# Two non-local attention layers in float32: who reads the products of a small matrix inverse out of PSUM

## The chip, the cores and the metric

The kernel runs on one core of one Trainium2 chip. The metric is the time of one execution on the device, in microseconds. All data are float32.

## The reference

Two layers of the same form follow each other on an image batch x of 4 x 128 x 96 x 96. Cut to what matters, one layer is:

```python
g_x = maxpool2(conv1x1(x, g_w, g_b))        # 64 channels, 2304 keys
theta_x = conv1x1(x, theta_w, theta_b)      # 64 channels, 9216 queries
phi_x = maxpool2(conv1x1(x, phi_w, phi_b))  # 64 channels, 2304 keys
attn = softmax(theta_x^T phi_x, over keys)
y = attn g_x
W_y = conv1x1(y, W_w, W_b)                  # back to 128 channels
inv = bn_gamma * rsqrt(bn_var + 1e-5)
return W_y * inv + (bn_beta - bn_mean * inv) + x
```

## The kernel before

**The work.** There are eight blocks (4 images, 2 layers), and each goes through its 9216 queries in nine pairs of 512 + 512. For a pair the kernel walks over 18 tiles of 128 keys: TensorE makes scores (`scores`, line L927, PSUM tile `sc`), ScalarE takes their exponential into SBUF (L932, `exp`), VectorE adds the exponentials up for the denominators (L939 and L941, `sum`), and TensorE multiplies them by the values (`values`, L949, PSUM tile `av`). One main loop runs over 648 *slots* `t`; a slot handles two key tiles, so nine slots make a pair, and 18 slots (`CYCLE`) are a cycle of two pairs. Each slot writes out, in this order: scores of tile 0, a piece of side work called `first`, scores of tile 1, a piece called `second`, the two additions to the sum, the values of the slot before, and then `closes`. Every engine runs its own instructions in the order written (no scheduler moves them).

**Side work.** Keys, values and queries of the next block are made beside the attention of the present one, by a `Unit` of eight steps `split`, `second` ... `eighth` at slots 8, 9, 11, 12, 14, 17, 20, 23 of a cycle (matmuls L685 and L694, PSUM tile `unit_ps`). Of interest below is `sixth_sum` (L764 to L771): three VectorE instructions, L766, L767, L770, read the two PSUM tiles of `sixth`. At slot 10 of a cycle a `theta_alone` also needs two PSUM tiles.

**The two banks.** All side work shares one PSUM pool, `ps_misc`, of two banks. `two_banks` hands out both at once, and whoever comes next on TensorE has to wait until the engine that reads the earlier products is done with them.

**The inverse.** The 128 x 64 projection W of each layer, scaled by the batch norm, has an upper 64 x 64 half A. `Fold` computes B = A^-1 times the other half by Newton's iteration, for both layers at once, 14 rounds, in slots 16 to 90, so that from the second block on the projection needs half the matmuls. One round is a `half` (V = I - A X / 2, one product per layer) and a `whole` (X = 2 c X V, four small products). Then come `first` (B = X times the right half), `residual`, `mended` (a correction of B), and `residual` again. `NEWTONS` lists the slots; at a listed slot, `whole` stands in the place of `first`, and the next `half` in `closes`, behind the values. In the profile the tiles of `Fold` carry the name `x`, since they are slices of the buffer of a later image.

Before, each `half` and each `whole` takes two new banks; ScalarE reads the products of `whole` (L379), and VectorE those of `half`, with the -0.5 and the identity in one instruction for each layer (L358). VectorE also reads the products of `residual` (L410) and `mended` (L416).

**W's loads.** `load_W` (L191 to L195) issues two DMAs on SyncE's queue for each layer, both layers ahead of the loop. VectorE scales W in `make_scale` (L210) at slot 9.

Of the kernel before, what the change touches and what calls it, by code (L numbers as in the profile page):

```python
# [11 lines left out]
AF = mybir.ActivationFunctionType  # L12
ALU = mybir.AluOpType
# [4 lines left out]
B, C, CI, H, W = 4, 128, 64, 96, 96  # L18
# [51 lines left out]
def shifted_blocks(ctx: ExitStack, tc: tile.TileContext, x: bass.AP, layers, out: bass.AP, flag):  # L70
# [24 lines left out]
    nc = tc.nc  # L95
# [17 lines left out]
    ident = const.tile([P, P], F32, name="ident")  # L113
# [5 lines left out]
    ones = const.tile([P, CI], F32, name="ones")  # L119
# [21 lines left out]
    def slice_of(n):  # L141
        used[0] += n
        return third[:, used[0] - n : used[0]]
# [154 lines left out]
    class Fold:  # L298


        def __init__(self):
            self.X = [slice_of(CI) for _ in range(2)]
            self.V, self.rest, self.square = (slice_of(CI) for _ in range(3))
            self.B = [slice_of(CI) for _ in range(2)]
# [13 lines left out]
        def squares(self, l):  # L318
            A = ws[l].W_bn[:CI, :]
            nc.vector.tensor_tensor(self.square[:CI, :], A, A, op=ALU.mult)  # L320
            nc.vector.tensor_reduce(self.total[:CI, l : l + 1], self.square[:CI, :], AX.X, ALU.add)
            nc.scalar.copy(self.X[l][ts(1 - l, CI), :], A)

        def begin(self, name):
            self.pss = two_banks(f"fold_ps_{name}")

        def scale(self):
            self.begin("scale")
            ps = self.pss[0][:, :2]
            for h in range(2):  # L330
                nc.tensor.matmul(
                    ps[ts(h, CI), :], lhsT=ones[:CI, :], rhs=self.total[:CI, :],
                    start=True, stop=True,
                )
            nc.vector.reciprocal(self.alpha, ps)

        def init(self):
            for l in range(2):
                own, other = self.own(l)
                for rows, src in ((own, self.left(l)), (other, self.X[l][other, :])):  # L340
                    nc.scalar.activation(
                        self.X[l][rows, :], src, AF.Identity, scale=self.alpha[rows, l : l + 1]
                    )
                nc.scalar.copy(self.own_alpha[own, :], self.alpha[own, l : l + 1])

        def half(self, k):

            def step():
                self.begin(f"half_{k}")
                for l in range(2):  # L350
                    own, other = self.own(l)
                    nc.tensor.matmul(
                        self.pss[l][other, :CI], lhsT=self.left(l), rhs=self.X[l][own, :],
                        start=True, stop=True,
                    )
                for l in range(2):
                    own, other = self.own(l)
                    nc.vector.scalar_tensor_tensor(  # L358
                        self.V[other, :], self.pss[l][other, :CI], -0.5, ident[other, other],
                        op0=ALU.mult, op1=ALU.add,  # L360
                    )

            return step

        def whole(self, k, c):

            def step():
                self.begin(f"whole_{k}")
                cols = ts(1, CI)
                for first in range(2):  # L370
                    for l in range(2):
                        own, other = self.own(l)
                        Xt, V = self.X[l][other, :], self.V[other, :]
                        rows, lhsT, rhs = ((own, Xt, V), (other, V, Xt))[first]
                        nc.tensor.matmul(
                            self.pss[1 - l][rows, cols], lhsT=lhsT, rhs=rhs, start=True, stop=True
                        )
                for l in range(2):
                    nc.scalar.activation(  # L379
                        self.X[l], self.pss[1 - l][:, cols], AF.Identity, scale=2.0 * c  # L380
                    )

            return step

        def product(self, name, rhs, take):

            def step():
                self.begin(name)
                for l in range(2):
                    own = ts(l, CI)  # L390
                    nc.tensor.matmul(
                        self.pss[l][:CI, :CI], lhsT=self.X[l][own, :], rhs=rhs(l),
                        start=True, stop=True,
                    )
                for l in range(2):
                    take(l, self.pss[l][:CI, :CI])

            return step

        def residual(self):  # L400
            self.begin("residual")
            cols = ts(1, CI)
            for l, w in enumerate(ws):
                nc.tensor.matmul(
                    self.pss[l][ts(l, CI), cols], lhsT=w.W_bn[:CI, :], rhs=self.B[l][:CI, :],
                    start=True, stop=True,
                )
# [4 lines left out]
        def first(self, l, ps):  # L412
            nc.scalar.copy(self.B[l][:CI, :], ps)

        def mended(self, l, ps):
            nc.vector.tensor_add(self.B[l][:CI, :], self.B[l][:CI, :], ps)  # L416
            for h in range(2):
                nc.scalar.copy(ws[l].B[ts(h, CI), :], self.B[l][:CI, :])

        def note(self):  # L420
            rest, big = self.rest, 2.0**40
# [16 lines left out]

        def steps(self):

            low, todo = NEWTON_LOW, []
            for k in range(NEWTON):
                c = 2.0 / (1.0 + low * (2.0 - low))
                low *= c * (2.0 - low)
                todo += [self.half(k), self.whole(k, c)]
            rest = lambda l: self.rest[ts(l, CI), :]
            todo += [self.product("first", self.right, self.first), self.residual]
            todo += [self.product("mended", rest, self.mended), self.residual]
            return todo

        def together(self):
            self.begin("together")
            nc.tensor.matmul(
                self.pss[0][:1, :1], lhsT=ones[:, :1], rhs=ones[:, :1], start=True, stop=True
            )

    def columns(wanted, name, engine, rows=None):
# [756 lines left out]
    ws = [Layer(l, p) for l, p in enumerate(layers)]  # L1214
# [76 lines left out]
    def then(t, step):  # L1291
        after[t] = after.get(t, []) + [step]

    fold = Fold()
# [32 lines left out]
    for n in range(1, len(blocks)):  # L1327
        first = (n - 1) * NP * NB // CYCLE * CYCLE
# [32 lines left out]
    todo = [None] + fold.steps()  # L1361
    for t in NEWTONS:
        assert is_free(t) and t not in firsts
        firsts[t], closes[t] = todo.pop(0), todo.pop(0) if todo else None
    assert not todo and t < (NP + 2) * NB + 3
    while not is_free(t + 1):
        t += 1
    firsts[t + 1] = fold.together
    then(t + 2, fold.note)
    then(t + 3, fold.note_growth)  # L1370

# [420 lines left out]
```

## Time and profile before

| | |
|---|---|
| median of three runs | 2483.23 us (lowest 2482.7) |
| the profiled execution's own time | 2483.54 us |
| its span | 2481.6 us |
| TensorE (PE) busy | 2450.8 us, 99% of the span |
| VectorE (DVE) busy | 2069.2 us, 83% |
| ScalarE (ACT) busy | 1675.5 us, 68% |
| GpSimd (POOL) busy | 900.0 us, 36% |
| granted TensorE clock, mean | 0.997 |

The span is the time from the first to the last instruction of the program; 1.94 us of the execution's own time lie around it. A busy share is an average over the whole kernel: where an engine with a share of 99% stood idle has to be found by stretches. In the lines of the profile PE is TensorE's matmul, PEld its weight load, and "L358" is line 358 of the kernel. A line of the timeline has the start in us, the duration in us, the engine, the source line, the operation, output and inputs, and the count; where an engine stood idle before it, the idle time and who ended it follow in brackets.

### The profile page before, as it was taken

The page shows a single profiled execution, that of the slowest core. Times are in us where ns is not written, and L with a number is a line of the kernel's source. Part 1 is how long each engine was busy: PE and PEld are TensorE (multiplying, and loading weights), DVE is VectorE, ACT ScalarE, POOL GpSimd, SP SyncE. Part 2 cuts the span into 40 slices and gives each one's busy share as a digit, 9 for nine tenths or more (in the row PEclk, how much of TensorE's full clock was granted, in tenths as well). Part 3 has the DMA queues.
Part 4 walks back from the last instruction along what each step waited for, and adds up shares of the span by engine and source line. Part 5 has one row for each costly group of instructions (what it writes and reads, how often), then busy time and mean ns, then how long its engine had stood idle before and what let it go on. Part 6 is the DMA issues. An engine that isn't in the chain of part 4 may idle for free.

```text
span 2481.6 us, 59305 instructions
## 1 busy us (share of the span) xinstructions
PE 2450.8 (99%) x23629; PEld 1035.0 (42%) x23629; DVE 2069.2 (83%) x2644; ACT 1675.5 (68%) x1929; POOL 900.0 (36%) x1033
## 2 busy tenths in 40 slices
PE   9999989999999999999999999999999999999999
PEld 3544544333333333333566664333333333333333
DVE  8887878898888888888878888888887888887777
ACT  6665656766666766666666666767666676766665
POOL 0222323433334433434434344443433444422331
PEclk9999999999999999999999999999999999999999
DMA  5555655766467776767756767776755677644443
GB/s 190 88 88 111 122 115 106 123 110 112 80 103 123 137 132 127 138 123 141 133 99 100 130 127 129 130 133 115 117 86 96 117 128 129 127 93 84 84 86 64
DMA packets 199629, 283.95 MB, mean 114 GB/s; under 512 B 36262, under 2 KB 131888, under 8 KB 199344
## 3 DMA queue, kind: packets, MB, share of 16 engines
q0 software_dynamic: 101872, 137.69, 42.5%
q1 hardware_dynamic: 97304, 142.31, 19.9%
q8 instruction: 188, 3.08, 0.5%
q14 instruction: 97, 0.79, 0.1%
q10 hardware_dynamic: 168, 0.07, 0.0%
HBM read 54.07 MB, written 35.68 MB: 36 GB/s over the span
## 4 chain that ended last, share of the span: by engine, by line
PE 91%; DVE 5%; issue 1%; DMA 1%; ACT 1%; POOL 0%; DVEq 0%; ACTq 0%; POOLq 0%
PE av L949 42%; PE sc L927 42%; PE unit_ps L685 5%; DVE sum L941 3%; PE W_ps L1096 1%; ACT exp L932 1%; DMA sums<-x 1%; PE unit_ps L694 0%; PE gphi_ps L542 0%; PE W_ps L1103 0%; PE mix_ps L844 0%; DVE gT L860 0%; DMA x<-in_x_dram 0%; PE theta_ps L904 0%; DMA sum<-turned 0%
## 5 line engine op out<-in xcount | busy, mean ns | idle before, releaser
L932 ACT ACTIVATE exp<-sc,nshift 128x1024 f32<-128x1024 f32 x1296 | 1402.5, 1115 | 746.4 <-PE sc L927 719.4
L941 DVE TENSOR_TENSOR sum<-sum,exp 128x1024 f32<-128x1024 f32 x1151 | 1407.8, 1223 | 300.3 <-ACT exp L932 247.0
L927 PE MATMUL sc<-theta,phi 64*64 64x512 f32 x10224 | 1291.1, 590 | 0.0
L949 PE MATMUL av<-exp,gT 64*64 64x512 f32 x10368 | 1257.2, 591 | 0.0
L949 PEld LDWEIGHTS av<-exp,gT 64*64 64x64 f32 x10368 | 458.5, 133 | 617.6 <-issue 572.4
L927 PEld LDWEIGHTS sc<-theta,phi 64*64 64x64 f32 x10224 | 450.7, 133 | 603.6 <-issue 536.6
L654 POOL DMA_DIRECT2D sums<-x x252 | 307.1, 1652 | 415.0 <-PE unit_ps L685 258.5
L1001 POOL DMA_DIRECT2D turned<-sum x140 | 115.2, 942 | 667.0 <-DMA turned<-sum 512.8
L1014 POOL DMA_DIRECT2D sum<-turned x280 | 263.7, 1492 | 42.0 <-DMA sum<-turned 35.8
L1113 POOL DMA_DIRECT2D x<-halves x122 | 101.1, 973 | 255.8 <-ACT halves L1111 246.7
L1127 POOL DMA_DIRECT2D x<-halves x122 | 149.2, 1651 | 39.8 <-ACT halves L1123 38.8
L685 PE MATMUL unit_ps<-sums,mixed 64*64 64x384 f32 x896 | 144.6, 484 | 10.1 <-DVE x L358 7.2
L939 DVE TENSOR_TENSOR sum<-exp,exp 128x1024 f32<-128x1024 f32 x72 | 88.2, 1224 | 46.1 <-ACT exp L932 46.0
L1083 POOL DMA_DIRECT2D halves<-halves x70 | 97.7, 1395 | 4.7 <-ACT halves L956 4.5
L956 ACT COPY halves<-av 128x1024 f32<-128x1024 f32 x71 | 72.0, 1013 | 32.1 <-PE av L949 31.7
L685 PEld LDWEIGHTS unit_ps<-sums,mixed 64*64 64x64 f32 x896 | 55.5, 133 | 73.6 <-issue 37.1
L685 PE MATMUL unit_ps<-x,mixed 64*64 64x384 f32 x448 | 71.0, 484 | 0.4 <-DVE stage L730 0.4
L654 POOL DMA_DIRECT2D sums<-sums x28 | 23.2, 830 | 81.4 <-PE unit_ps L694 29.4
L1123 ACT ACTIVATE halves<-W_ps,shift 128x256 f32<-128x256 f32 x122 | 51.3, 480 | 0.0
L1088 DVE TENSOR_TENSOR halves<-halves 128x512 f32<-128x512 f32 x71 | 48.6, 685 | 0.0
L685 PE MATMUL unit_ps<-sums,gphiT 64*64 64x384 f32 x224 | 46.3, 483 | 0.0
L805 DVE TENSOR_REDUCE pooled_g<-stage 128x96 f32<-128x384 f32 x84 | 45.9, 546 | 0.0
(196 smaller groups left out, 1069.1 us busy)
## 6 DMA issues: line engine op xcount, KB each, us to landing
sums<-x POOLq DMA_DIRECT2D x252, 192.0 KB, 5.4
x<-halves POOLq DMA_DIRECT2D x244, 128.0 KB, 4.4
sums<-x SPq DMA_DIRECT2D x112, 192.0 KB
turned<-sum SPq DMA_DIRECT2D x140, 128.0 KB
turned<-sum POOLq DMA_DIRECT2D x140, 128.0 KB, 3.7
halves<-halves POOLq DMA_DIRECT2D x70, 256.0 KB, 5.5
halves<-row SPq DMA_DIRECT2D x140, 128.0 KB
out_dram<-x SPq DMA_DIRECT2D x35, 512.0 KB
```

The source lines that it names most:

```text
L654: return lambda: nc.gpsimd.dma_start(out=dst(), in_=src(), accum_op=ALU.add)
L685: nc.tensor.matmul(bank[ts(c, CI), :UN], lhsT=lhsT, rhs=rhs[:, c, :], start=True, stop=True)
L927: nc.tensor.matmul(ps[ts(c, CI), ts(h, QT)], lhsT=self.blk.keys_of(k, c, h), rhs=self.th[ts(h, CI), :], start=True, stop=True,)
L932: nc.scalar.activation(e, ps, AF.Exp, bias=nshift)
L939: nc.vector.tensor_add(self.sum, self.es[0], e)
L941: nc.vector.tensor_add(self.sum, self.sum, e)
L949: nc.tensor.matmul(self.av[ts(h, CI), ts(r, QT)], lhsT=self.blk.gT[ts(r, CI), k, :], rhs=e[ts(r, CI), ts(h, QT)], start=(k == 0), stop=(k ...
L1001: nc.gpsimd.dma_start(out=self.turned[ts(h, CI)], in_=self.sum[ts(h, CI), ts(h, QT)], accum_op=ALU.add,)
L1014: nc.gpsimd.dma_start(out=folded()[ts(i, SQ)], in_=self.turned[ts(i, SQ), ts(k, n)], accum_op=ALU.add,)
L1083: nc.gpsimd.dma_start(out=self.y, in_=self.halves[:, QT:], accum_op=ALU.add)
L1113: nc.gpsimd.dma_start(out=here[:CI, h, :], in_=top[ts(h, CI), :], accum_op=ALU.add)
L1127: nc.gpsimd.dma_start(out=here[CI:, :, ts(c, n)], in_=self.y[ts(c, CI), :].rearrange("p (h n) -> p h n", h=2), accum_op=ALU.add,)
```

## The change

- `half` has one bank's part for both layers. ScalarE takes the two products out of PSUM in one instruction, times -0.5, into V, and VectorE adds the identity to V later, from SBUF (`eye`, a copy of the identity made once).
- `whole` and the `half` behind it in the same slot share one pair of banks (`whole` the first 64 columns, `half` the second 64 of one of them); `begin` is called once a slot.
- `residual` and `mended` are read by ScalarE too, and VectorE does its addition from SBUF.
- The last steps are spread over one more slot, 94: residual at 88, correction and copies (`keep`) at 90, last residual at 94.
- Layer 1's `load_W` is issued in slot 4 of the loop.

```diff
-NEWTONS = (16, 18, 22, 25, 34, 36, 43, 52, 54, 58, 61, 70, 72, 79, 82, 88, 90)
+NEWTONS = (16, 18, 22, 25, 34, 36, 43, 52, 54, 58, 61, 70, 72, 79, 82, 88, 90, 94)
...
-        def half(self, k):
...
-                for l in range(2):
-                    own, other = self.own(l)
-                    nc.vector.scalar_tensor_tensor(
-                        self.V[other, :], self.pss[l][other, :CI], -0.5, ident[other, other],
-                        op0=ALU.mult, op1=ALU.add,
-                    )
...
+        def half(self):
+
+            ps = self.pss[1][:, ts(1, CI)]
+            for l in range(2):
+                own, other = self.own(l)
+                nc.tensor.matmul(
+                    ps[other, :], lhsT=self.left(l), rhs=self.X[own, l, :], start=True, stop=True
+                )
+            nc.scalar.activation(self.V, ps, AF.Identity, scale=-0.5)
+            nc.vector.tensor_add(self.V, self.V, self.eye)
...
         def residual(self):
...
+            nc.scalar.activation(self.rest, ps, AF.Identity, scale=-1.0)
             for l in range(2):
                 own = ts(l, CI)
-                nc.vector.tensor_sub(self.rest[own, :], self.right(l), self.pss[l][own, cols])
...
+                nc.vector.tensor_add(self.rest[own, :], self.rest[own, :], self.right(l))
+
+        def mended(self):
+            more = self.X[:CI]
+            self.product(lambda l: self.rest[ts(l, CI), :], more)
+            nc.vector.tensor_add(self.B[:CI], self.B[:CI], more)
+
+        def keep(self):
+            for l, w in enumerate(ws):
+                for h in range(2):
+                    nc.scalar.copy(w.B[ts(h, CI), :], self.B[:CI, l, :])
...
-    for w in ws:
-        w.load_W(nc.sync)
+    ws[0].load_W(nc.sync)
...
+    then(4, lambda: ws[1].load_W(nc.sync))
...
         if t in firsts:
             assert first is None and second is None
+            fold.begin(t)
             first = firsts[t]
```

TensorE, from the `half` at the end of slot 34 to the `sixth` of slot 35, with what each row waits for. Before:

```order
L352 MATMUL fold_ps_half_0_1616<-x_111,WT_620 64x64 [waits Activation_49]
L352 MATMUL fold_ps_half_1_1617<-x_111,WT_629 64x64 [waits Activation_49]
L927 MATMUL sc_0_3_16_1624<-theta_0_3_1019,phi_0_151 64x512 x4
L685 MATMUL unit_ps_0_1_0_1631<-sums_104,mixed_277 64x384 [waits DMASW6_49,DVE_49]
L685 MATMUL unit_ps_0_1_1_1632<-x_268,mixed_277 64x384 [waits DVE_49]
```

The same place after the change:

```order
L353 MATMUL fold_ps_1_1581<-x_111,WT_622 64x64 [waits Activation_49]
L353 MATMUL fold_ps_1_1581<-x_111,WT_631 64x64 [waits Activation_49]
L915 MATMUL sc_0_3_16_1618<-theta_0_3_1019,phi_0_149 64x512 [waits PE_49]
L915 MATMUL sc_0_3_16_1618<-theta_0_3_1019,phi_0_149 64x512 x3
L673 MATMUL unit_ps_0_1_0_1625<-sums_104,mixed_277 64x384 [waits DMASW6_49,PE_49]
L673 MATMUL unit_ps_0_1_1_1626<-x_266,mixed_277 64x384 [waits Activation_49]
```

The order of the matmuls is the same; the first matmuls of `sixth` waited for VectorE, which had `half`'s banks, and now wait for ScalarE.

ScalarE in slots 34 to 36, before:

```order
L932 ACTIVATE exp_0_3_14_1589<-sc_0_3_14_1584,nshift 128x1024
L379 ACTIVATE x_111<-fold_ps_whole_1_1592 128x64
L379 ACTIVATE x_111<-fold_ps_whole_0_1591 128x64
L932 ACTIVATE exp_0_3_15_1604<-sc_0_3_15_1599,nshift 128x1024
L932 ACTIVATE exp_0_3_16_1629<-sc_0_3_16_1624,nshift 128x1024
```

and after:

```order
L920 ACTIVATE exp_0_3_14_1587<-sc_0_3_14_1582,nshift 128x1024
L371 ACTIVATE x_111<-fold_ps_1_1581 128x64
L371 ACTIVATE x_111<-fold_ps_0_1580 128x64
L920 ACTIVATE exp_0_3_15_1600<-sc_0_3_15_1595,nshift 128x1024
L356 ACTIVATE x_111<-fold_ps_1_1581 128x64
L920 ACTIVATE exp_0_3_16_1623<-sc_0_3_16_1618,nshift 128x1024
```

One short instruction, L356, stands now between the second exponential of slot 34 and the first of slot 35.

VectorE in slots 34 and 35, before:

```order
L941 TENSOR_TENSOR sum_0_3_1337<-sum_0_3_1337,exp_0_3_15_1604 128x1024
L358 SCALAR_TENSOR_TENSOR x_111<-fold_ps_half_0_1616,ident 64x64
L358 SCALAR_TENSOR_TENSOR x_111<-fold_ps_half_1_1617,ident 64x64
L805 TENSOR_REDUCE pooled<-stage 128x96
L941 TENSOR_TENSOR sum_0_3_1337<-sum_0_3_1337,exp_0_3_16_1629 128x1024
L766 TENSOR_TENSOR stage<-stage,unit_ps_0_1_1_1632 128x384
L767 SCALAR_TENSOR_TENSOR stage<-unit_ps_0_1_0_1631,cols_first,stage 128x384
L770 TENSOR_TENSOR stage<-stage,unit_ps_0_1_0_1631 128x384
```

and after:

```order
L929 TENSOR_TENSOR sum_0_3_1333<-sum_0_3_1333,exp_0_3_15_1600 128x1024
L357 TENSOR_TENSOR x_111<-x_111 128x64
L793 TENSOR_REDUCE pooled<-stage 128x96
L929 TENSOR_TENSOR sum_0_3_1333<-sum_0_3_1333,exp_0_3_16_1623 128x1024
L754 TENSOR_TENSOR stage<-stage,unit_ps_0_1_1_1626 128x384
L755 SCALAR_TENSOR_TENSOR stage<-unit_ps_0_1_0_1625,cols_first,stage 128x384
L758 TENSOR_TENSOR stage<-stage,unit_ps_0_1_0_1625 128x384
```

One instruction stands in the place of two, and no longer reads PSUM. The `sixth_sum` (L766 to L770, now L754 to L758) still reads both banks of `sixth` behind it, and the `whole` of slot 36 needs those banks.

More of the change, by code (lines that the diff above doesn't have):

```diff
@@ L301, in __init__ @@
         def __init__(self):
-            self.X = [slice_of(CI) for _ in range(2)]
-            self.V, self.rest, self.square = (slice_of(CI) for _ in range(3))
-            self.B = [slice_of(CI) for _ in range(2)]
+            self.X, self.B = (
+                slice_of(2 * CI).rearrange("p (l c) -> p l c", l=2) for _ in range(2)
+            )
+            self.V, self.rest, self.square, self.eye = (slice_of(CI) for _ in range(4))
+            for h in range(2):
+                nc.scalar.copy(self.eye[ts(h, CI), :], ident[ts(h, CI), ts(h, CI)])
             self.alpha, self.own_alpha, self.total = slice_of(2), slice_of(1), slice_of(2)
@@ L321, in squares @@
             nc.vector.tensor_reduce(self.total[:CI, l : l + 1], self.square[:CI, :], AX.X, ALU.add)
-            nc.scalar.copy(self.X[l][ts(1 - l, CI), :], A)
+            nc.scalar.copy(self.X[ts(1 - l, CI), l, :], A)
         def begin(self, name):
@@ L372, in step @@
                         own, other = self.own(l)
-                        Xt, V = self.X[l][other, :], self.V[other, :]
+                        Xt, V = self.X[other, l, :], self.V[other, :]
                         rows, lhsT, rhs = ((own, Xt, V), (other, V, Xt))[first]
                         nc.tensor.matmul(
-                            self.pss[1 - l][rows, cols], lhsT=lhsT, rhs=rhs, start=True, stop=True
+                            self.pss[1 - l][rows, :CI], lhsT=lhsT, rhs=rhs, start=True, stop=True
                         )
@@ L379, in step, with product @@
                     nc.scalar.activation(
-                        self.X[l], self.pss[1 - l][:, cols], AF.Identity, scale=2.0 * c
+                        self.X[:, l, :], self.pss[1 - l][:, :CI], AF.Identity, scale=2.0 * c
                     )
             return step
[L385 to L403, printed above, removed]
+        def product(self, rhs, to):
+            pss = [self.pss[1 - l][:CI, ts(1, CI)] for l in range(2)]
+            for l in range(2):
                 nc.tensor.matmul(
-                    self.pss[l][ts(l, CI), cols], lhsT=w.W_bn[:CI, :], rhs=self.B[l][:CI, :],
+                    pss[l], lhsT=self.X[ts(l, CI), l, :], rhs=rhs(l),
                     start=True, stop=True,
@@ L408, in residual, with first @@
             for l in range(2):
-                own = ts(l, CI)
-                nc.vector.tensor_sub(self.rest[own, :], self.right(l), self.pss[l][own, cols])
[L412 to L418, printed above, removed]
+                nc.scalar.copy(to[:, l, :], pss[l])
+        def first(self):
+            self.product(self.right, self.B[:CI])
+        def residual(self):
+            ps = self.pss[0][:, :CI]
+            for l, w in enumerate(ws):
+                nc.tensor.matmul(
+                    ps[ts(l, CI), :], lhsT=w.W_bn[:CI, :], rhs=self.B[:CI, l, :],
+                    start=True, stop=True,
+                )
+            nc.scalar.activation(self.rest, ps, AF.Identity, scale=-1.0)
+            for l in range(2):
+                own = ts(l, CI)
+                nc.vector.tensor_add(self.rest[own, :], self.rest[own, :], self.right(l))
[4 more added lines that the diff above has]
+        def keep(self):
+            for l, w in enumerate(ws):
+                for h in range(2):
+                    nc.scalar.copy(w.B[ts(h, CI), :], self.B[:CI, l, :])
         def note(self):
@@ L439, in steps @@
         def steps(self):
-            low, todo = NEWTON_LOW, []
+            low, todo = NEWTON_LOW, [self.half]
             for k in range(NEWTON):
@@ L444, in steps @@
                 low *= c * (2.0 - low)
[L445 to L449, printed above, removed]
+                todo += [self.whole(c), self.half if k + 1 < NEWTON else self.first]
+            return todo + [self.residual, None, self.mended, self.keep, self.residual]
         def together(self):
-            self.begin("together")
             nc.tensor.matmul(
-                self.pss[0][:1, :1], lhsT=ones[:, :1], rhs=ones[:, :1], start=True, stop=True
+                self.pss[1][:1, :1], lhsT=ones[:, :1], rhs=ones[:, :1], start=True, stop=True
             )
@@ L1360, in shifted_blocks @@
     firsts, closes = {15: fold.scale}, {15: fold.init}
-    todo = [None] + fold.steps()
+    todo = [None] + fold.steps() + [fold.together]
     for t in NEWTONS:
         assert is_free(t) and t not in firsts
-        firsts[t], closes[t] = todo.pop(0), todo.pop(0) if todo else None
+        firsts[t], closes[t] = todo.pop(0), todo.pop(0)
     assert not todo and t < (NP + 2) * NB + 3
-    while not is_free(t + 1):
-        t += 1
-    firsts[t + 1] = fold.together
     then(t + 2, fold.note)
```

19 lines of the change are left out of this document (4 added, 15 removed).

## The prediction

> **What bounds the kernel now.** I read the busy shares first, then the same shares by stretch, and then TensorE's own timeline for the places where it stood idle.
>
> ```profile
> PE 2450.8 (99%) x23629; PEld 1035.0 (42%) x23629; DVE 2069.2 (83%) x2644; ACT 1675.5 (68%) x1929; POOL 900.0 (36%) x1033
> ...
> 60.00:440.00 380.00, 357.73 (x3474) 177.59 (x3470) 313.76 (x480) 238.71 (x311) 111.48 (x127) 0.98 0.57 105
> 440.00:2420.00 1980.00, 1979.23 (x19156) 814.11 (x19152) 1657.92 (x1999) 1362.75 (x1522) 772.95 (x881) 1.00 0.65 116
> ```
>
> The columns of the stretches are length, then busy time of PE, PEld, DVE, ACT and POOL, and the granted clock. From 440 us on TensorE is busy 1979.23 of 1980 us at clock 1.00: nothing that takes work from another engine can help there. From 60 to 440 us, which holds the inverse, it is idle for 380.00 - 357.73 = 22.27 us, and the clock is 0.98. So whatever this change is worth must come out of that stretch. These are TensorE's idle times in it (one more, 0.44 us at 67 us, lies before the inverse):
>
> ```profile
> 88.73 0.53 PE L685 MATMUL unit_ps<-sums,mixed 64*64 64x384 f32 x1 [2.29 <-DVE x L358]
> 115.44 1.12 PE L685 MATMUL unit_ps<-sums,mixed 64*64 64x384 f32 x8 [0.47 <-DVE x L358]
> 128.56 0.38 PE L694 MATMUL unit_ps<-x,mixed 64*64 64x192 f32 x2 [1.47 <-DVE x L358]
> 166.54 0.53 PE L685 MATMUL unit_ps<-sums,mixed 64*64 64x384 f32 x1 [1.45 <-DVE x L358]
> 207.17 0.58 PE L694 MATMUL unit_ps<-x,mixed 64*64 64x192 f32 x2 [4.66 <-DVE x L358]
> 247.55 0.53 PE L685 MATMUL unit_ps<-sums,mixed 64*64 64x384 f32 x1 [1.47 <-DVE x L358]
> 272.57 1.12 PE L685 MATMUL unit_ps<-sums,mixed 64*64 64x384 f32 x8 [0.48 <-DMA sum<-turned]
> 285.35 0.38 PE L694 MATMUL unit_ps<-x,mixed 64*64 64x192 f32 x2 [1.14 <-DVE x L358]
> 322.81 0.53 PE L685 MATMUL unit_ps<-sums,mixed 64*64 64x384 f32 x1 [1.47 <-DVE x L358]
> 362.72 0.38 PE L694 MATMUL unit_ps<-x,mixed 64*64 64x192 f32 x2 [4.81 <-DVE x L358]
> 401.73 0.53 PE L685 MATMUL unit_ps<-sums,mixed 64*64 64x384 f32 x1 [1.65 <-DVE x L416]
> 406.64 0.27 PE L404 MATMUL fold_ps_residual<-x 64*64 64x64 f32 x1 [0.47 <-DVE stage L770]
> ```
>
> In slot order these are slots 17, 23, 26, 35, 44, 53, 59, 62, 71, 80, 89 and 90: each the slot right behind a `half` (or behind `mended`). TensorE wants the two banks, and VectorE, which works its additions off in order, has not yet read `half`'s products. The one named a DMA (slot 59) has the size of its twin in slot 23 (0.48 and 0.47), also behind a `half`; I count it with them. The twelve sum to 21.83 us.
>
> Idle time has a second price. Behind the three longest the granted clock falls:
>
> ```profile
> 90.00:94.00 4.00, 4.00 (x28) 2.25 (x23) 3.97 (x9) 1.11 (x1) 0.94 (x1) 0.57 0.49 106
> 206.00:214.00 8.00, 6.83 (x44) 2.89 (x48) 3.66 (x5) 1.55 (x3) 0.00 (x0) 0.57 0.45 147
> 363.00:367.00 4.00, 4.00 (x32) 1.67 (x28) 2.05 (x2) 1.54 (x3) 0.00 (x0) 0.57 0.73 246
> 126.00:131.00 5.00, 3.53 (x43) 1.55 (x40) 3.71 (x5) 2.11 (x2) 0.56 (x1) 1.00 0.40 90
> ```
>
> A clock of 0.57 over 4 us is a loss of 4 x 0.43 = 1.7 us of work. The three cost 1.7, 8 x 0.43 - 1.17 / 2 = 2.9 (the 1.17 idle us inside did no work anyway), and 1.7: together 6.3 us. Behind the 1.47 us at 128.56 (last row) the clock stayed at 1.00.
>
> The Trainium skill ("TensorE: Matmul & The Clock Gate", section "HAM oscillation — how this bites in real kernels") puts the limit at idle gaps of more than about 3.4 us. By it the 2.29 us of slot 17 would have kept the full clock and the second price would be 1.7 us smaller; the row at 90 us says 0.57, so here the trace decides.
>
> **The change, term by term.** I take one place, slots 34 to 36, on VectorE and then on TensorE.
>
> ```profile
> 163.68 2.54 DVE L941 TENSOR_TENSOR sum<-sum,exp 128x1024 f32<-128x1024 f32 x2
> 166.26 0.48 DVE L358 SCALAR_TENSOR_TENSOR x<-fold_ps_half,ident 64x64 f32<-64x64 f32 x2
> 166.66 0.54 DVE L805 TENSOR_REDUCE pooled<-stage 128x96 f32<-128x384 f32 x1
> ...
> 168.25 0.54 DVE L766 TENSOR_TENSOR stage<-stage,unit_ps 128x384 f32<-128x384 f32 x1
> ...
> 169.24 0.54 DVE L770 TENSOR_TENSOR stage<-stage,unit_ps 128x384 f32<-128x384 f32 x1
> ...
> 164.06 1.03 PE L927 MATMUL sc<-theta,phi 64*64 64x512 f32 x5
> ...
> 167.24 1.28 PE L927 MATMUL sc<-theta,phi 64*64 64x512 f32 x8
> ...
> 169.81 1.28 PE L927 MATMUL sc<-theta,phi 64*64 64x512 f32 x8
> 170.67 0.27 PE L375 MATMUL fold_ps_whole<-x 64*64 64x64 f32 x2
> ```
>
> *Removed: the wait for L358.* TensorE runs out of scores at 164.06 + 1.03 = 165.09, and VectorE frees the bank at 166.54, behind two sums. ScalarE will free it instead. Its instruction is like the L379 that reads `whole` today (below, 226 ns), and in its queue stands only the exponential of the slot's second score tile, whose scores end 1.7 us of values earlier; the exponential behind it needs scores that TensorE makes after `half`. So the bank should be free about 0.3 us after `half` ends, inside the 0.86 us of scores that TensorE has left (169.81 to 170.67). I cost the 14 new ScalarE instructions at nothing; uncovered they would be 14 x 0.226 = 3.2 us, which I keep for the upper end.
>
> Each wait also costs a restart. Eight scores normally follow on each other in 0.86 us, two fours of 0.43, while the last four is listed with 0.59, so idle time is counted 0.16 us late; and the first four after the wait come in two steps, 0.25 apart. I take 0.2 us a wait. Twelve waits: 21.83 + 2.4 + 6.3 (clock) = **30.5 us** lie on the path now.
>
> *Given back: the next bank.* In slots 17, 35, 53, 71 and 89 the matmuls are those of `sixth`, and in the next slot `whole` (or `mended`) needs the banks that VectorE's L766 to L770 read. TensorE now comes earlier, but VectorE hardly does: it works without a pause from 163.68 to 169.78 and saves only its two L358, 0.40 us to the start of L805, against one addition from SBUF. The nearest row to that addition has the same shape:
>
> ```profile
> L379 ACT ACTIVATE x<-fold_ps_whole x28: 210/226/237, 96.0 to 373.7; 128x64 f32<-128x64 f32 x28
> ...
> L433 DVE TENSOR_TENSOR x<-BT x2: 216/218/221, 421.9 to 422.5; 128x64 f32<-128x64 f32 x2
> ```
>
> 218 ns as listed, somewhat less from start to start; I take 0.26 us saved (between 0.18 and 0.40). Today `whole` comes 170.67 - 166.54 = 4.13 us behind `sixth`. Without the wait `sixth` starts at 166.54 - 1.45 - 0.2 = 164.89 and `whole` is wanted at 169.02. L770 ends at 169.24 + 0.54 - 0.26 = 169.52, and 0.05 later (the distance from L358's end to the matmul) TensorE can go: 0.55 us of waiting, where 1.65 were. The other four places go by the same sum:
>
> ```profile
> 91.43 0.54 DVE L770 TENSOR_TENSOR stage<-stage,unit_ps 128x384 f32<-128x384 f32 x1
> ...
> 250.25 0.54 DVE L770 TENSOR_TENSOR stage<-stage,unit_ps 128x384 f32<-128x384 f32 x1
> ...
> 325.51 0.54 DVE L770 TENSOR_TENSOR stage<-stage,unit_ps 128x384 f32<-128x384 f32 x1
> ...
> 403.90 1.23 DVE L941 TENSOR_TENSOR sum<-sum,exp 128x1024 f32<-128x1024 f32 x1 [1.63 <-ACT exp L932]
> ...
> 406.04 0.55 DVE L770 TENSOR_TENSOR stage<-stage,unit_ps 128x384 f32<-128x384 f32 x1
> ```
>
> Slot 18: `whole` wanted at 88.73 - 2.49 + 4.13 = 90.37, free at 91.76: 1.4 us. Slots 54 and 72: wanted at 250.01 and 325.27, free at 250.58 and 325.84: 0.6 each. Slot 90: wanted at 401.73 - 1.85 + 4.13 = 404.01; L770 comes earlier by the 1.63 us in which VectorE waits for an exponential (ScalarE's copies of B no longer stand ahead of it) and by about 0.4 for L416 and L410, so free at about 404.6: 0.6 us. Together **3.7 us** come back, none long enough for the clock by the rows above.
>
> At `split` (slots 26, 44, 62, 80) and `eighth` (23, 59) nothing comes back: the bank behind them is read by ScalarE, or wanted two or more slots later. VectorE is late there, as the two waits near 4.7 us tell, but from 440 us on the same steps run with VectorE 84% busy and TensorE without a pause. With TensorE 4.9 us earlier in slot 44 I find `second_sum` of slot 45 done about 1.6 us before `theta_alone` wants its bank in slot 46, and in slot 81 about 1.1 us before `whole` of slot 82. That is the cover; each us beyond it would come back.
>
> *Moved and added elsewhere.* Fifteen score tiles now wait for a TensorE event, that of the matmul two key tiles back in the same buffer, long past: nothing. The two copies of `eye`, two ScalarE reads in `residual` and two in `mended` lie in ScalarE's 32% of idle time; `keep` puts four copies (about 1 us) between exponentials in slot 90, as `mended` did in 88. W of layer 1 moves on SyncE's queue behind loads that wait for the next image:
>
> ```profile
> 33.13 3.06 SPq L651 DMA_DIRECT2D sums<-x  x4
> ...
> 60.76 0.26 DVE L210 TENSOR_SCALAR x<-x,inv 128x64 f32<-128x64 f32 x1
> ```
>
> It will be issued near 35 us, and is first read at 60.76: some 25 us for 64 KB, nothing lost. The next image's load is issued a little under 1 us earlier, which no wait of TensorE shows a use for.
>
> **Sum.** 30.5 - 3.7 = 26.8 us off the profiled 2483.54 us: 2456.7, so **2457 us**. The median (2483.23) is 0.3 us from the profiled run, and I make no correction. That is 1.1% less, inside the 2% which I take as what a measurement of this kernel can tell from no change.
>
> **Rivals.**
> 1. *The wait moves in full.* If VectorE is no earlier at L770, or the restart costs more, the five places behind `sixth` give all their time back: 2.29 + 1.45 + 1.47 + 1.47 + 1.65 + 5 x 0.2 + 1.7 (clock at slot 17) = 11.0, while the others still gain 30.5 - 11.0 = 19.5: 2464 us. For it: VectorE is without a pause there. Against it: it would have to lose the 1.1 us that TensorE does not wait in slot 35.
> 2. *Nothing comes back,* if VectorE gets ahead by more than I count: 2483.5 - 30.5 = 2453 us. Against it: five rows of L770.
> 3. *Half clock behind what is left.* The 1.4 us in slot 18 lie between gaps that kept the clock (1.47) and one that lost it (2.29). A fall there costs 1.7 us more: 2458 us. The Trainium skill (the same page, section "Part 1: The HAM clock gate (the "warmup" mystery)") has a free-running window of about 3.4 us, by which the same gap may or may not lose the clock; the rows here cannot tell.
> 4. *W comes late, and it is slower.* SyncE works in order, and W stands behind the `sums` loads. If it landed after 60.8 us, VectorE would stop in `make_scale` with the exponentials' sums queued behind, TensorE would follow once the five exponential buffers are full, and each further us would cost one. To eat the gain of 26.8 it would have to land near 60.8 + 27 = 88 us; at 95 the time would be 2490. From 35 us on that is 60 us for 64 KB. Against it: SyncE is idle from 36 us on.
>
> **Chances.** Forecast with its give-back 0.68, rival 1 0.14, rival 2 0.08, rival 3 0.05, rival 4 0.02, something unseen 0.03. The range takes in rivals 1 to 3 with the unknown ends: low 2453 less 1 for the spread between runs, 2452; high 2464 + 3.2 (ScalarE's instructions uncovered), 2467. None of the cases reaches 2433.6, the mark of 2% faster: 0.01; slower by over 2% needs W 50 us later still: 0.01; within 2% 0.98.
>
> **What will show it.** After the change the stretch 60 to 440 us (now ending near 413) should have about 3 to 4 us of idle time on TensorE in five places, all at a `whole` or `mended` behind `sixth`, released by VectorE's L758, and none released by the new L357. The clock should stay at 1.00 through it. ScalarE's L356 should start within 0.2 us of the end of `half`. I am wrong if waits for ScalarE's L356 appear (an exponential held it up), if waits behind `split` move to slot 46 or 82, or if VectorE stops near 60 us.

## The result, and the profile after

The changed kernel takes **2455.85 us** (median of four runs), the kernel before 2484.38 us in the same comparison: a ratio of **0.9888**, with a 95% interval of 0.9869 to 0.9908. It is 1.1% faster, and 2457 was forecast. Each of the two medians counts one execution that took far longer than the rest (6744.94 and 3711.95 us); without them they are 2454.84 and 2483.23 us. The profiled execution took 2454.51 us, with a span of 2452.6.

The busy shares, and below them the two stretches that the forecast began with:

```profile
PE 2442.0 (100%) x23629; PEld 989.9 (40%) x23629; DVE 2064.4 (84%) x2629; ACT 1677.3 (68%) x1949; POOL 899.8 (37%) x1033
```

```profile
60.00:440.00 380.00, 377.47 (x3758) 219.71 (x3754) 332.93 (x493) 262.57 (x354) 125.55 (x143) 1.00 0.64 115
440.00:2420.00 1980.00, 1979.18 (x19140) 737.05 (x19136) 1657.90 (x2001) 1358.80 (x1516) 763.73 (x871) 1.00 0.64 114
206.00:214.00 8.00, 8.00 (x84) 6.23 (x80) 7.86 (x14) 5.13 (x6) 4.53 (x5) 1.00 0.62 84
```

In the stretch of the inverse TensorE is now idle for 380.00 - 377.47 = 2.53 us, where it was 22.27, and its clock is 1.00 instead of 0.98 (the third row is a stretch of time in which 0.57 stood before; the changed kernel is further on in its work there). From 440 us on TensorE is busy without a pause in both, 1979.18 and 1979.23 us of 1980. That alone does not say that the work there takes equally long; the starts of the exponentials below do.

The view of waits sums up who released TensorE there. First the kernel before, then the changed one; the columns are the total in us, the number of waits, and the longest:

```profile
PE unit_ps L694 <- DVE x L358: 12.1, 4, 4.8
PE unit_ps L685 <- DVE x L358: 7.2, 5, 2.3
PE unit_ps L685 <- DVE x L416: 1.6, 1, 1.6
PE unit_ps L685 <- DMA sum<-turned: 0.5, 1, 0.5
PE fold_ps_residual L404 <- DVE stage L770: 0.5, 1, 0.5
PE unit_ps L685 <- DVE stage L730: 0.4, 1, 0.4
```

```profile
PE fold_ps L367 <- DVE stage L758: 1.3, 4, 0.7
PE fold_ps L380 <- DVE stage L758: 0.7, 1, 0.7
PE unit_ps L673 <- DVE stage L718: 0.4, 1, 0.4
```

The 0.4 us at L673 (once L685) lie at 67 us, before the inverse. All waits for `half`'s reader are gone, and the five that were forecast have come, at a `whole` (L367) or `mended` (L380) behind the last read of `sixth_sum` (L758, once L770). The two new instructions are in the groups by line:

```profile
L356 ACT ACTIVATE x<-fold_ps 128x64 f32<-128x64 f32 x14 | 3.2, 225 | 4.1 <-PE fold_ps L353 4.1
L357 DVE TENSOR_TENSOR x<-x 128x64 f32<-128x64 f32 x14 | 3.1, 221 | 2.1 <-ACT x L356 2.1
```

Both last what the forecast took from their neighbours (226 and 218 ns), and no wait of TensorE's matmuls names either.

Where the time went can be followed slot by slot, by the start of a slot's first exponential in the two traces. These rows are slot 16, slot 100 and the last slot, 647, before and after:

```profile
83.64 1.11 ACT L932 ACTIVATE exp<-sc,nshift 128x1024 f32<-128x1024 f32 x1
...
444.82 1.12 ACT L932 ACTIVATE exp<-sc,nshift 128x1024 f32<-128x1024 f32 x1
...
2465.15 1.12 ACT L932 ACTIVATE exp<-sc,nshift 128x1024 f32<-128x1024 f32 x1 [0.45 <-PE sc L927]
```

```profile
83.44 1.11 ACT L920 ACTIVATE exp<-sc,nshift 128x1024 f32<-128x1024 f32 x1
...
415.74 1.12 ACT L920 ACTIVATE exp<-sc,nshift 128x1024 f32<-128x1024 f32 x1
...
2436.29 1.12 ACT L920 ACTIVATE exp<-sc,nshift 128x1024 f32<-128x1024 f32 x1 [0.46 <-PE sc L915]
```

The changed kernel is 0.2 us ahead at slot 16 and 29.1 at slot 100, so the inverse is 28.9 us shorter. At slot 647 it is 28.9 ahead: behind the inverse the work takes as long as before to 0.2 us, and the whole gain lies in the inverse. The same subtraction at each place between:

| wait removed in slot | idle before, us | time saved, us | returned at the next `whole` or `mended`, us |
|---|---|---|---|
| 17 | 2.29 | 4.46 (with 1.7 of clock) | 1.45 |
| 23, 59 | 0.47, 0.48 | 0.94, 0.94 | none |
| 26, 62 | 1.47, 1.14 | 1.76, 1.39 | none |
| 35, 53, 71 | 1.45, 1.47, 1.47 | 1.91, 1.92, 1.92 | 0.59 each |
| 44, 80 | 4.66, 4.81 | 7.84, 6.75 (with 2.9 and 1.7 of clock) | none |
| 89, 90 | 1.65, 0.47 | 2.46, 1.26 | 1.36 |
| sum | 21.83 | 33.55 | 4.58 |

That leaves 28.97; shifts of up to 0.4 us elsewhere, which nearly cancel, make up the rest to 28.9. The forecast had 30.5 and 3.7.

### The profile page after: what moved, and what is told of

Same layout as the page of the kernel before. It is cut to its first block, busy times and chain, and to the rows that moved or that the text cites. A ratio compares the mean times of both kernels' runs of the same rounds, so it can differ in the third digit from the quotient of the medians.

```text
span 2452.6 us, 59312 instructions
## 1 busy us (share of the span) xinstructions
PE 2442.0 (100%) x23629; PEld 989.9 (40%) x23629; DVE 2064.4 (84%) x2629; ACT 1677.3 (68%) x1949; POOL 899.8 (37%) x1033
## 4 chain that ended last, share of the span: by engine, by line
PE 93%; DVE 4%; DMA 1%; issue 1%; ACT 1%; POOL 0%; DVEq 0%; ACTq 0%
PE sc L915 43%; PE av L937 43%; PE unit_ps L673 5%; DVE sum L929 2%; PE W_ps L1084 1%; DMA sums<-x 1%; ACT exp L920 1%; PE gphi_ps L530 0%; PE unit_ps L682 0%; PE W_ps L1091 0%; PE mix_ps L832 0%; PE theta_ps L892 0%; DMA x<-in_x_dram 0%; DVE sum L927 0%; PE gphi_ps L476 0%
## 5 line engine op out<-in xcount | busy, mean ns | idle before, releaser
L937 PEld LDWEIGHTS av<-exp,gT 64*64 64x64 f32 x10368 | 436.6, 133 | 634.8 <-issue 592.1
L915 PEld LDWEIGHTS sc<-theta,phi 64*64 64x64 f32 x10224 | 427.7, 133 | 627.8 <-issue 556.5
L673 PE MATMUL unit_ps<-sums,mixed 64*64 64x384 f32 x896 | 142.1, 483 | 0.8 <-DMA sums<-x 0.7
L673 PEld LDWEIGHTS unit_ps<-sums,mixed 64*64 64x64 f32 x896 | 53.0, 133 | 60.2 <-issue 36.2
L673 PE MATMUL unit_ps<-x,mixed 64*64 64x384 f32 x448 | 71.7, 483 | 0.4 <-DVE stage L718 0.4
L673 PE MATMUL unit_ps<-sums,gphiT 64*64 64x384 f32 x224 | 46.8, 482 | 0.0
L793 DVE TENSOR_REDUCE pooled<-stage 128x96 f32<-128x384 f32 x84 | 45.9, 546 | 0.0
```

Of the source, the lines that this page charges most:

```text
L673: nc.tensor.matmul(bank[ts(c, CI), :UN], lhsT=lhsT, rhs=rhs[:, c, :], start=True, stop=True)
L915: nc.tensor.matmul(ps[ts(c, CI), ts(h, QT)], lhsT=self.blk.keys_of(k, c, h), rhs=self.th[ts(h, CI), :], start=True, stop=True,)
L937: nc.tensor.matmul(self.av[ts(h, CI), ts(r, QT)], lhsT=self.blk.gT[ts(r, CI), k, :], rhs=e[ts(r, CI), ts(h, QT)], start=(k == 0), stop=(k ...
```

## The experiments

**1. Of the whole change only `half`: ScalarE reads it, out of one bank.** Does the bank pair that `whole` and `half` share matter, or who reads?

```diff
 # the kernel before; whole, residual, mended, slots and W as before
-                        self.pss[l][other, :CI], lhsT=self.left(l), rhs=self.X[l][own, :],
+                        self.pss[1][other, :CI], lhsT=self.left(l), rhs=self.X[l][own, :],
...
-                    nc.vector.scalar_tensor_tensor(
-                        self.V[other, :], self.pss[l][other, :CI], -0.5, ident[other, other],
-                        op0=ALU.mult, op1=ALU.add,
-                    )
+                nc.scalar.activation(self.V, self.pss[1][:, :CI], AF.Identity, scale=-0.5)
+                nc.vector.tensor_add(self.V, self.V, self.eye)
```

> The kernel before with one edit: `half` puts both products into one of its two banks, ScalarE reads them out in one instruction, and VectorE adds the identity from SBUF. `whole`, `residual`, `mended`, the slots and W's load stay as before. Theory (VectorE's late read of `half` is the cost): the waits in slots 17, 23, 26, 35, 44, 53, 59, 62, 71 and 80 go, with the clock that falls behind three of them; in slots 89 and 90 waits of about 1.65 and 0.47 us stay, since VectorE still reads `mended`. From the exponentials' starts in the two traces, the ten slots gave 29.9 us in the changed kernel and the `whole` of slots 18, 36, 54 and 72 took 3.2 back: 26.7 us less than before, about 2457 to 2458 us, within 3 us of the changed kernel. Rival (the shared bank pair of `half` and `whole`, with one request for banks a slot, is what pays): within 5 us of before, about 2484.

Measured: **2457.24 us** against 2483.21 (ratio 0.9898, 0.9882 to 0.9913). Its waits in the inverse:

```profile
PE unit_ps L683 <- DVE x L414: 1.6, 1, 1.6
PE fold_ps_whole L373 <- DVE stage L768: 1.3, 4, 0.7
PE fold_ps_residual L402 <- DVE stage L768: 0.5, 1, 0.5
...
PE fold_ps_whole L373 <- DVE stage L764: 0.2, 1, 0.2
```

No wait for `half` is left, and the two at the end, where VectorE still reads `mended`, are as they were. By the starts of the exponentials both kernels gain 26.9 us up to slot 88, so the bank pair shared with `whole`, and the one request for banks a slot, add nothing that shows. Up to slot 95 this kernel still gains 26.9 us and the changed one 28.9: the new end is worth 2.0 us. The edit changes two things at once, the reader and the number of banks; run 2 takes them apart.

**2. Only the reader of `half` is changed back.**

```diff
 # the changed kernel
-            nc.scalar.activation(self.V, ps, AF.Identity, scale=-0.5)
-            nc.vector.tensor_add(self.V, self.V, self.eye)
+            nc.vector.scalar_tensor_tensor(
+                self.V, ps, -0.5, self.eye, op0=ALU.mult, op1=ALU.add
+            )
```

> The changed kernel with one edit undone: VectorE reads `half` out of PSUM again, now in one instruction for both layers (-0.5 times the products plus `eye`), and its addition from SBUF goes. The shared bank pair, `residual`, `mended`, `keep`, slot 94 and W's place stay as changed. Theory (VectorE's late read of `half`): the ten waits come back, 19.7 us idle in the trace less up to 0.25 us at some places for the second read that is gone, with the half clock behind the longest: about 2456 + 26 = 2482 us (2478 to 2485). Rival (the shared bank pair pays): 2456 to 2462.

Measured: **2475.48 us** (ratio 0.9965, 0.9952 to 0.9979). This fits neither: the waits come back, but smaller, and the time is 6.5 us under the 2482 of my theory. Beside the changed kernel, from which only the reader differs, it loses 19.6 us.

```profile
PE unit_ps L683 <- DVE x L356: 7.0, 3, 3.5
PE unit_ps L674 <- DVE x L356: 5.2, 6, 1.6
PE fold_ps L381 <- DVE stage L759: 0.6, 1, 0.6
```

That is 12.2 us of waiting for `half`'s reader, where the kernel before had 19.3 by its own rows. The timeline of TensorE at slot 44 shows how:

```profile
200.72 0.38 PE L683 MATMUL unit_ps<-x,mixed 64*64 64x192 f32 x2
...
205.48 0.38 PE L683 MATMUL unit_ps<-sums,mixed 64*64 64x192 f32 x2 [3.36 <-DVE x L356]
```

The first matmuls of `split` run at 200.72 and only the second ones wait. In the changed kernel `half` fills one of the two banks, so the other is free for the next step, and whatever scores stand between the two halves of that step run too. But one reading instruction of VectorE is gone as well. The next run puts both back.

**3. As 2, with `half` in both banks.**

```diff
 # the changed kernel
-            ps = self.pss[1][:, ts(1, CI)]
...
+                nc.tensor.matmul(
+                    self.pss[l][other, ts(1, CI)], lhsT=self.left(l), rhs=self.X[own, l, :],
+                    start=True, stop=True,
+                )
...
+                nc.vector.scalar_tensor_tensor(
+                    self.V[other, :], self.pss[l][other, ts(1, CI)], -0.5, ident[other, other],
+                    op0=ALU.mult, op1=ALU.add,
+                )
```

> The changed kernel with `half` read by VectorE as before and with its two products in both banks again, each read by an instruction of its own; the one request for banks a slot, the end of the inverse and W's place stay as changed. Theory (with VectorE as the reader, the products' lying in one bank shortens TensorE's wait, since the first matmuls of the next step go into the free bank): the waits are those of the kernel before again, 2.3, 1.5, 4.7 and 4.8 us in slots 17, 26, 44 and 80, and the time is the kernel before's less the 2 to 3 us of the end, about 2481 us. Rival (the second reading instruction or the separate requests for banks made the difference of the run with VectorE and one bank): waits of 1.7, 0.2, 3.4 and 3.5 us as there, and 2475 us.

Measured: **2480.51 us** (ratio 0.9992, 0.9982 to 1.0002; the kernel before 2482.67).

```profile
PE unit_ps L686 <- DVE x L358: 12.1, 4, 4.8
PE unit_ps L677 <- DVE x L358: 7.1, 5, 2.3
```

The waits for `half` are those of the kernel before to 0.1 us. So the free bank and the second reading instruction are together worth 5.0 us by the medians (2480.51 to 2475.48), and 6.7 by the starts of the exponentials, as long as VectorE is the late reader. The run puts both back and cannot divide them. These rows of slot 17 bound the instruction's part:

```profile
88.40 0.90 PE L677 MATMUL unit_ps<-sums,mixed 64*64 64x384 f32 x1 [2.30 <-DVE x L358]
88.65 0.90 PE L677 MATMUL unit_ps<-x,mixed 64*64 64x384 f32 x1
```

The first matmul starts behind the first read and the one for the other bank 0.25 us later, behind the second. My estimate from this is at most 0.25 us for each of ten waits, 2.5 us; the free bank has the rest, at least 4 of the 6.7 us, of which 4.6 stand at the four places of `split`. What a free bank is worth once ScalarE reads, no run here shows, since run 1 has it too.

**4. VectorE reads, but earlier in its queue.** Is VectorE's reading slow, or its place in the queue late?

```diff
 # the kernel of 2, in outline; in the slots of half, and in 82, 88, 90 and 94
-        add_ups()                  # the slot's two additions to the sum
         ... values of the slot before ...
         if closes.get(t):
             closes[t]()            # half, and VectorE's read of it
+        add_ups()
```

> The changed kernel with `half` read by VectorE in one instruction, and that instruction, in the slots of `half` alone, ahead of the slot's two additions to the sum instead of behind them. Theory (TensorE waits for the reader's place in VectorE's queue, not for how VectorE reads PSUM): the read comes 2.5 us earlier in the queue, so the waits of slots 17, 23, 26, 35, 53, 62 and 71 go, those of slots 44 and 80, 3.4 and 3.5 us with VectorE behind the sums, shrink to about 0.8 us, the sums come up to 1.6 us later where VectorE waits for `half`, and the time is about 2458 us (2455 to 2464). Rival (VectorE as the reader costs the time wherever it stands): 2472 to 2476 us.

Measured: **2460.73 us** (ratio 0.9915, 0.9897 to 0.9933). VectorE at slot 16, and TensorE's waits:

```profile
85.38 0.21 DVE L356 SCALAR_TENSOR_TENSOR x<-fold_ps,x 128x64 f32<-128x64 f32 x1
85.51 2.54 DVE L930 TENSOR_TENSOR sum<-sum,exp 128x1024 f32<-128x1024 f32 x2
```

```profile
PE fold_ps L368 <- DVE stage L759: 2.7, 4, 0.7
PE unit_ps L683 <- DVE x L356: 2.0, 2, 1.1
PE fold_ps L381 <- DVE stage L759: 0.7, 1, 0.7
```

The same instruction on the same engine, 2.5 us further forward, regains 14.8 of the 19.6 us between run 2 and the changed kernel. So it is the queue. What is left is as expected too: slots 44 and 80 wait (0.94 and 1.07 us), and VectorE, which now stands still for `half`, is later at each read of `sixth`, so that four `whole` wait 2.7 us in all instead of 1.3.

**5. Only the move of W's load.**

```diff
 # the kernel before
-    for w in ws:
-        w.load_W(nc.sync)
+    ws[0].load_W(nc.sync)
...
+    then(4, lambda: ws[1].load_W(nc.sync))
```

> The kernel before with one edit: layer 1's `load_W` is issued in slot 4 of the loop. Theory (the load was never waited for, and nothing behind it on SyncE's queue gains): the same as before within 1 us, 2484. Rival (the images' loads, issued earlier without it, or W's later arrival, move the start of the loop): a difference that grows before slot 10, of 2 us or more either way.

Measured: **2482.92 us** against 2483.21 (ratio 0.9999, 0.9990 to 1.0008). The move neither costs nor brings anything that a time can show.

**6. `whole` away from `sixth_sum`.** The five waits that are left all stand where a `whole` or `mended` comes in the slot behind `sixth`. Other free slots avoid four of them.

```diff
-NEWTONS = (16, 18, 22, 25, 34, 36, 43, 52, 54, 58, 61, 70, 72, 79, 82, 88, 90, 94)
+NEWTONS = (16, 22, 24, 34, 43, 52, 54, 58, 61, 70, 73, 79, 82, 88, 91, 94, 97, 100)
```

> The changed kernel with other slots for the inverse: 16, 22, 24, 34, 43, 52, 54, 58, 61, 70, 73, 79, 82, 88, 91, 94, 97, 100, so that `whole` or `mended` stands right behind the reads of `sixth_sum` only in slot 54. Theory (what was given back is a wait for VectorE's last read of `sixth_sum` in slots 18, 36, 72 and 90, 1.4 + 0.6 + 0.6 + 1.4 us with the restarts by the exponentials' starts): these waits go, nothing takes their place, and the time is about 4 us under the changed kernel, 2452 us; the trace shows one wait of about 0.2 us at a `whole`, in slot 54. Rival (VectorE is late everywhere in this stretch, so that other bank users wait instead): as much idle time on TensorE as in the changed kernel, some 2 us in other slots, and 2456 us.

Measured: **2451.66 us** (ratio 0.9873, 0.9858 to 0.9888). The only waits left in the stretch are these, the first of which lies before the inverse:

```profile
PE unit_ps L673 <- DVE stage L718: 0.4, 1, 0.4
PE fold_ps L367 <- DVE stage L758: 0.2, 1, 0.2
```

No other wait took their place. Beside the changed kernel on the same chip:

> The changed kernel once more, as the standard for the run beside it: 2455 to 2457 us, waits of 0.67, 0.19, 0.19, 0.26 and 0.65 us at the matmuls behind `sixth_sum`, and no fall of the clock.

> The changed kernel with the later slots for `whole` once more, beside the changed kernel on the same chip. Theory (four of the five waits for `sixth_sum` are gone, which cost 3.8 us by the starts of the exponentials): 3 to 5 us under the changed kernel, a ratio of 0.998 to it. Rival (the difference between the two earlier medians, 2455.85 and 2451.66, was that of two chips): within 1 us of it.

The changed kernel took 2456.32 us (2453.73 to 2457.97), this one **2451.11** (2450.76 to 2451.81), with ratios to the kernel before of 0.9889 (0.9873 to 0.9906) and 0.9871 (0.9854 to 0.9887): 5.2 us, 0.2%. The runs do not overlap, though the two intervals do. By the starts of the exponentials the inverse is 3.3 us shorter in this pair of runs and in the earlier one (from slot 16 to slot 104, where both are done; the 3.8 of the expectation was read at slot 95, ahead of the last steps, which now come later). Behind 440 us TensorE waited for DMAs of the images' sums 2.3 us in the one profiled execution and 0.8 in the other, which adds 1.5 us to the difference of these two. It is the fastest of the kernels here.

**7. Waits of chosen length.** ScalarE copies a scratch tile some times ahead of the read of `half`, so that TensorE has to wait for it.

```diff
 # the changed kernel, in ten of the slots with a half
+            for n, wide in zip(DIAL.get(self.at, ()), (256, 128)):
+                for _ in range(n):
+                    nc.scalar.copy(self.idle[:, :wide], self.idle[:, :wide])
             nc.scalar.activation(self.V, ps, AF.Identity, scale=-0.5)
```

> The changed kernel with idle copies on ScalarE ahead of the read of `half` in ten slots (16, 22, 25, 34, 43, 52, 58, 61, 70, 79): 4, 10, 6, 14, 8, 18, 8, 12, 6 and 16 copies of 128x256 and a few of 128x128, an estimate of 0.3 us each. What it measures is what a wait of TensorE costs beyond its listed idle time. Expected idle times: 0.5 to 1.1, 2.7, 1.5, 4, 2, 5, 2.3, 3.2, 1.7 and 4.5 us. Theory (a restart costs 0.2 to 0.45 us a wait, and the half clock comes when a stretch of the clock's 3.41 us grid holds about 1.9 us of idle time or more, so that waits of 1.9 to 3.8 us lose it or not by where they fall): waits from 4 us on always lose it, those under 1.7 never, and the time is about 2492 to 2500 us. Rival 1 (length alone decides, somewhere between 1.5 and 2.3 us): all from 2.3 us on lose it. Rival 2 (idle time under 3.4 us never loses it): only the three longest do.

> As the run with 4 to 18 idle copies on ScalarE ahead of the read of `half`, with the lengths dealt to the ten slots in another order: 16, 6, 12, 8, 18, 4, 14, 8, 10 and 6 copies of 128x256. Theory (the place on the clock's 3.41 us grid decides for waits of 1.9 to 3.8 us): a wait of the same middle length loses the full clock in one run and not in the other, and each loss is worth 1.7 us. Rivals: by length alone, or only from 3.4 us on, both runs show the same lengths with and without a loss. The time of the two runs agrees within 5 us by all of them.

Measured: 2497.85 and 2499.22 us, one run each. The first lists these waits in the inverse:

```profile
PE unit_ps L680 <- ACT x L363: 19.4, 6, 6.1
PE unit_ps L689 <- ACT x L363: 9.2, 4, 4.6
```

28.6 us of idle time made it 42.0 us longer, 40.4 of them in the inverse by the starts of the exponentials. That is net: the four waits of `whole` behind `sixth`, which cost the changed kernel 3.0 us in this subtraction, are gone. So waiting costs about half as much again as the idle time says. Two things make up the difference. Ten waits of the two runs lie outside any clock loss. At `split` (L689) four of them cost 0.55, 0.55, 0.56 and 0.59 us beyond their idle time, at `eighth` (L680) two cost 0.21. At `sixth` (L680) three cost 0.18, and this is 0.72 less the 0.54 us that the `whole` behind them no longer waits; in slot 17, where that is 1.40, the wait of 0.87 us costs less than its idle time. The rest is the clock, and there length alone does not decide. Two waits of the first run, and the windows around them:

```profile
280.44 0.55 PE L680 MATMUL unit_ps<-sums,mixed 64*64 64x384 f32 x3 [2.99 <-ACT x L363]
...
295.88 0.57 PE L689 MATMUL unit_ps<-sums,mixed 64*64 64x192 f32 x2 [2.87 <-ACT x L363]
```

```profile
275.45:278.87 3.42, 2.00 (x24) 0.79 (x17) 2.06 (x2) 3.23 (x8) 2.85 (x4) 1.00 0.85 137
278.87:282.28 3.41, 1.84 (x20) 1.23 (x24) 1.79 (x8) 2.48 (x7) 0.00 (x0) 1.00 0.37 60
282.28:285.69 3.41, 3.41 (x37) 2.21 (x33) 3.31 (x6) 1.95 (x2) 0.00 (x0) 1.00 0.30 92
292.52:295.93 3.41, 0.54 (x9) 0.06 (x4) 0.28 (x2) 3.19 (x10) 0.00 (x0) 1.00 0.96 190
295.93:299.35 3.42, 3.42 (x20) 2.19 (x24) 2.54 (x3) 2.33 (x4) 0.00 (x0) 0.50 0.43 177
```

The wait of 2.99 us is cut by a boundary at 278.87 into 1.42 and 1.57 us of idle time, and the clock stays at 1.00. The wait of 2.87 us falls into one window, in which TensorE works for 0.54 us, and the next window runs at 0.50. Rival 1 (length alone) falls with this pair, and rival 2 (nothing under 3.4 us) with the second wait. In the second run waits of 2.84 and 2.87 us lost the full clock, and one of 2.64 kept it.

## Why the prediction was right, point by point

- *What bounds the kernel.* Right: the gain lies in the inverse alone. The lead is 29.1 us at slot 100 and 28.9 at slot 647.
- *The removed wait for VectorE.* Right, and shown from both sides: run 1 brings nearly the whole gain by the edit of `half` alone, run 2 loses 19.6 us of it when only the reader is undone, and run 3 nearly all when VectorE reads two banks again. Run 4 shows that it is the place in the queue.
- *Its size.* 30.5 us were forecast, and 33.6 measured by the table. The mis-sized term is the restart. I named two parts of it, 0.16 us by which idle time is counted late and 0.25 us by which the first four scores come in two steps, and then took 0.2 a wait. The seven waits of the table without a clock loss, up to slot 71, cost 0.25 to 0.47 us beyond their idle time, 0.40 in the mean: about the sum of the two parts. Over twelve waits that is 2.4 us more; the remaining 0.6 us lies in the last two, slots 89 and 90, which cost 0.8 each beyond it. The second part is the 0.25 us between VectorE's two reads of `half` (the rows under run 3).
- *The clock.* The 6.3 us are what the profiled execution lost, but not a constant of the kernel. Run 5 has the same waits as the kernel before, and its clock did not fall behind slot 17; in slots 17 and 44 it is 2.5 us quicker for that alone. With run 5's profile, the term would have been about 4.
- *Given back.* All five places were right, and 3.7 us were forecast; 4.6 came by the table, 1.45, 3 x 0.59 and 1.36. Slots 18, 36, 54 and 72 came within 0.06 us of the working; slot 90 was put at 0.6, and why it cost 1.36 the runs leave open. Run 6 takes four of the five away and gains 3.3 us by the starts of the exponentials. The idle times listed, 0.19 to 0.67 us, are less than what the places cost: the first products of `whole` start on the bank that L754 frees (in slot 18 L754 ends at 90.43 us and the first product starts at 90.48), and only the others wait for L758.
- *ScalarE's read within 0.2 us of `half`'s end.* Right in ten places (0.08 us), wrong in slots 18, 36, 54 and 72, where the copy of a finished pair stood ahead of it:

```profile
166.51 1.01 ACT L944 COPY halves<-av 128x1024 f32<-128x1024 f32 x1 [0.60 <-PE fold_ps L353]
167.42 0.23 ACT L356 ACTIVATE x<-fold_ps 128x64 f32<-128x64 f32 x1
```

  I had listed only the exponential as being ahead. The read is 0.9 us late there and costs nothing: `theta_alone`, which also stands in slot 1 of a cycle, takes the bank at 167.98, 0.33 us behind it.
- *W's load.* It was issued at 33.1 us (35 forecast), and `make_scale` read W at 60.58:

```profile
33.10 0.60 SPq L193 DMA_DIRECT2D x<-in_L_conv_W_w_dram  x1
```

```profile
60.58 0.26 DVE L210 TENSOR_SCALAR x<-x,inv 128x64 f32<-128x64 f32 x1
```

- *The rivals.* 1 (the wait moves in full) and 2 (nothing comes back) fall with the five short waits; 3 (half clock at slot 18) did not come, and its 1.4 us did not lie between the gaps that it was compared with, 1.47 and 2.29, but under both; 4 (W late) falls with run 5. The net of the inverse, 28.9 us, is 2.1 more than the 26.8 forecast: 3.0 by the removal, less 0.9 given back. That the recorded median is only 1.15 us from the forecast is in part luck: two terms were too small, and their errors stand against each other.

What I did not see in the diff is the finding of runs 2 and 3: putting `half` into one bank, read by one instruction, would by itself have saved about 5 us of what VectorE's lateness cost. ScalarE's read makes the wait vanish anyway, so I take it that this adds little to it; that is argued and not run.

## What to carry to other kernels

When the bounding engine waits for a buffer, look at what stands ahead of the reader in its queue: here the same instruction on the same engine, placed 2.5 us earlier, gave three quarters of what another engine gave. When such a wait goes, go to the next user of the same buffer and compare its old distance with the reader's; that sum found all five places where time came back, and moving those users away gained another 3.3 us. Count a wait at more than its listed idle time, here 0.4 us more each in the mean and 0.2 to 0.8 by place, and treat the part due to the clock as something that differs from execution to execution.

## What the runs showed of the hardware

The half clock comes on a fixed grid of time. In every trace here the falls of the granted clock within the loop last 3.41 or 6.83 us, and their starts in one trace lie whole multiples of 3.413 us apart. The fall goes with the idle time within one window of that grid. Laid on TensorE's rows in six traces (the kernel before and those of runs 2, 3, 5 and 7), it gives over 70 windows with more than 0.4 us of idle time: windows at full clock with up to 1.57 us of idle time kept it, and with 2.08 us or more lost it in the next window. Between these both occur. The kernel before and the kernel of run 5 have the same wait at the same place of the grid, 1.51 us of work in the window, and differ in the clock behind it (the granted clock is the third column from the end):

```profile
86.83:90.24 3.41, 1.51 (x16) 1.07 (x20) 3.24 (x6) 0.84 (x1) 0.09 (x1) 1.00 0.24 82
90.24:93.65 3.41, 3.41 (x23) 1.94 (x18) 3.41 (x7) 1.11 (x1) 0.85 (x1) 0.50 0.54 116
```

```profile
86.90:90.32 3.42, 1.51 (x16) 1.07 (x20) 3.25 (x6) 0.84 (x1) 0.09 (x1) 1.00 0.26 77
90.32:93.73 3.41, 3.41 (x44) 2.33 (x39) 3.41 (x7) 1.43 (x2) 0.84 (x1) 1.00 0.56 121
```

Once the clock is half, less idle time keeps it there: in the same traces 0.88 us or more within the first half-clock window led to a second one, and 0.62 or less to none. The Trainium skill ("TensorE: Matmul & The Clock Gate", section "Part 1: The HAM clock gate (the "warmup" mystery)") has a free-running window of 3413 ns, and the lengths and distances of the falls here agree with it. Its section "HAM oscillation — how this bites in real kernels" has the clock fall for idle gaps over some 3.4 us; here gaps of 1.65 us (run 2, slot 17), 2.29 and 2.87 lost it, and one of 2.99 kept it.
